# First two stages: whole-image evictions, the bias behind the convolution, rows by h mod 4, and every queue in program order

## The chip, the cores and the metric

The kernel runs on one core of a Trainium2 chip. The metric is the device time of one execution in microseconds (us).

## What is computed

The input is x, 16 images of 192 channels and 64x64 pixels, f32. Two layers follow each other:

```python
# layer 0
h = layernorm_over_channels(x) * w + b
projected, gate = split(conv1x1(h, 192 -> 384) + bias)
projected = depthwise3x3(projected)                    # zero padding
scanned = four recurrences s = d*s + (1-d)*cur of projected: along w, both ways, and along h, both ways, weighted by a softmax
local = depthwise3x3(projected)                        # other taps
mixed = (scanned + local) * sigmoid(gate)
bn = batchnorm(mixed)                                  # statistics over images and pixels
x = x + conv1x1(gelu(bn), 192 -> 192)
x = x + conv1x1(gelu(conv1x1(layernorm(x), 192 -> 768)), 768 -> 192)
# layer 1
t = relu(norm(mean_over_pixels(x) @ w1.T)); taps = t @ w2.T
out = depthwise 3x3 convolution of x with the image's own taps (four of nine) + bias
```

## The kernel before

A short **setup** (L73 to L195) computes the constants on the chip. Among them are the projection's weights with the norm's scale folded in and the channel mean taken out (wi), the bias broadcast over the partitions (bias_bc), the decay of each channel (dec_b), and for each channel the rows of the banded matrices that do a convolution or a recurrence along w as a matmul. The rows go to HBM (dv_d by L192, lv_d by L194, both on SP) and are read back in stage B shifted, as matrices.

**Stage A** (L197 to L265) is the layernorm's statistics and the 192 to 384 projection. Two images are worked on at once, one on partitions 0 to 63 and one on 64 to 127. An iteration takes 512 pixels of each, which is eight image rows in four groups of 128; there are 64 iterations, and four of them fill a block of 16 row pairs. load_a (L208) brings x in two DMAs of 384 KB on SP, two iterations ahead into three buffers. stat_a (L218) transposes 12 tiles on TensorE and takes mean and variance of each pixel on VectorE (L228, L229), then a root on ScalarE and a reciprocal. project (L235) does 12 matmuls of 384 columns in a group (L243) and evicts both images' results from one PSUM tile ps_pj (two of them in turn): the 192 projected channels by VectorE with the norm's factor and the bias (L246, the helper's line is L64), the 192 gate channels by ScalarE (L247). Both write every 16th element of a staging tile. After four iterations POOL's queue stores the staging tiles with four DMAs of 64 partitions (L252), 24 KB in one run for each partition. pg_d holds, for each image and row block, w, then the channel, then 16 rows of one parity of h.

**Stage B** (L268 to L398) goes through 24 groups of eight channels, four pairs in each; all 16 images are there at once, eight on each half of the partitions (partition = w). load_b (L285) brings a group's projected and gate values and its matrices, all on SP, one group ahead, in runs of 512 B. For a pair: depthwise (L305, seven parts with their edge cases, since rows lie by parity; 56 matmuls), copy from PSUM by ScalarE (q, L331), two decay tables by ScalarE (tab, L339), two scans along h by VectorE (L343, L345), local convolution and scans along w by matmuls (L352), sigmoid by ScalarE (L373), product and statistics by VectorE (L377, L378), and every four pairs a store by POOL's queue (L382). Then the batch norm's factors are made (L402 to L437), and the weights of stage C are loaded (L440 to L478).

**Stage C** (L481 to L695) has 64 chunks of 512 pixels of two images, in a software pipeline. load (L515) brings the chunk's x (two DMAs on SP, L520, two buffers) and, for every even chunk, y, the mixed values of two chunks (eight DMAs on SP, L528, one buffer). unmix transposes y on VectorE (L539), bn_gelu is L544 and L545 on ScalarE, out_proj multiplies and adds x on VectorE (L552, t = 0 to 2; the PSUM tile "a" has one buffer and is shared with the means ps_m and ps_v), center and normalize are the second layernorm (L563 to L581), first and second are the two large projections (L591 and L506, with gelu L594), final adds the result (L612). dynamic (L644 to L655) does layer 1 in pieces of 16 rows, and POOL's queue stores them.

What sets the order: Tile derives the waits and, on engines that are not named in manual_schedule, also the order of instructions in a block, by planned times. In stages A and B only TensorE keeps the order of the program (PE_ORDER, L62); in stage C TensorE, VectorE and ScalarE do. SP and POOL, whose queues only issue DMAs here, are ordered by the planner in all three. The loop of stage C starts:

```python
for n in range(-3, n_ch + 2):
    ...
    at(load, n + 3)
    at(unmix, n + 3)
    at(first, n, 0)
    at(bn_gelu, n + 3)
    at(out_proj, n + 2, 0)
    ...
    at(out_proj, n + 2, 2)
    at(second, n, 1)
```

Of the kernel before, what the change touches and what calls it, by code (L numbers as in the profile page):

```python
# [43 lines left out]
AR = CR // 2  # L44

# [7 lines left out]
def conv_block_kernel(ctx: ExitStack, tc: tile.TileContext, x, prm, w_in, w_out, w_fc1, b_fc1, w_fc2, w1, bn1, w2, out):  # L53
# [7 lines left out]
    PE_ORDER = {mybir.EngineType.PE}  # L61
# [14 lines left out]
    pg_d = dram.tile([n_img_all, NB, HW, 2 * C * BR], F32, tag="pg_d", name="pg_d")  # L76
# [7 lines left out]
    load_cls3(pt3, prm)  # L84

# [6 lines left out]
    eps5 = cp.tile([128, 1], F32, tag="eps5", name="eps5")  # L92
    nc.vector.memset(eps5, 1e-5)
# [3 lines left out]
    bias_bc = ce.tile([128, 2 * C], F32, tag="bias_bc", name="bias_bc")  # L97
    dec_b = ce.tile([128, 2, C // 2], F32, tag="dec_b", name="dec_b")
    stats = ce.tile([128, C, 6], F32, tag="stats", name="stats")


    with ExitStack() as stage:
        ka = stage.enter_context(tc.tile_pool(name="ka", bufs=1))
        wi = ka.tile([128, 3, 2 * C], F32, tag="wi", name="wi")
        load_cls3(wi, w_in)

        with tc.tile_pool(name="ps_set", bufs=1, space=PSUM) as ps0, tc.tile_pool(name="sset", bufs=1) as sp:
            lo = slice(0, 64)

# [21 lines left out]
            dg = sp.tile([64, 3, 4, 64], F32, tag="dg", name="dg")  # L131
            lnb = sp.tile([64, 3, 128], F32, tag="lnb", name="lnb")
            for t in range(3):
                for k, v in enumerate((pt3[lo, t, INB:INB + 1], pt3[lo, t, GTB:GTB + 1], dec[:, t, 2:3], dec[:, t, 3:4])):
                    nc.vector.tensor_scalar_mul(dg[:, t, k], ident[lo, lo], v)
                nc.vector.tensor_scalar_mul(lnb[:, t], ones[lo], pt3[lo, t, LN1B:LN1B + 1])
            pb = ps0.tile([128, 2 * C], F32, tag="pb", name="pb")
            for t in range(3):
                nc.tensor.matmul(pb, lnb[:, t], wi[lo, t], start=(t == 0), stop=False)
            for t in range(3):  # L140
                for k in range(2):
                    c0 = k * C + 64 * t
                    nc.tensor.matmul(pb[:, c0:c0 + 64], ones[lo], dg[:, t, k], start=False, stop=(t == 2 and k == 1))
            nc.vector.tensor_copy(bias_bc, pb)
            pd = ps0.tile([128, 2, C], F32, tag="pd", name="pd")
            for t in range(3):
                for k in range(2):
                    nc.tensor.matmul(pd[:, k, 64 * t:64 * t + 64], ones[lo], dg[:, t, 2 + k],
                                     start=(t == 0 and k == 0), stop=(t == 2 and k == 1))

            for i, q in enumerate(HALF):
                nc.vector.tensor_copy(dec_b[q].rearrange("p k (g c) -> p k g c", c=GC // 2),
                                      pd[q].rearrange("p k (g i c) -> p k g i c", i=2, c=GC // 2)[:, :, :, i])


            for t in range(3):
                nc.vector.tensor_scalar_mul(wi[:, t], wi[:, t], pt3[:, t, LN1W:LN1W + 1])
# [3 lines left out]
            for t in range(3):  # L161
                nc.tensor.matmul(pc, mean_w, wi[lo, t], start=(t == 0), stop=(t == 2))
            for t in range(3):
                nc.vector.tensor_sub(wi[:, t], wi[:, t], pc)
# [20 lines left out]
            gt = sp.tile([128, 8, C], F32, tag="gt", name="gt")  # L185
# [5 lines left out]
            for k in range(3):  # L191
                nc.sync.dma_start(dv_d[:, k].rearrange("g s c -> s g c"), gt[:, k].rearrange("s (g c) -> s g c", c=GC))  # L192
            for k in range(5):
                nc.sync.dma_start(lv_d[:, :, k].rearrange("g i s c -> s (g i) c"),  # L194
                                  gt[:, 3 + k].rearrange("s (g c) -> s g c", c=GC // 2))  # L195

        xp = stage.enter_context(tc.tile_pool(name="xa", bufs=3))  # L197
# [6 lines left out]
        xr = x.rearrange("b (t p) h w -> b p t (h w)", p=64)  # L204
# [3 lines left out]
        def load_a(n):  # L208
            p, c = divmod(n, NCH)
            xa = xp.tile([128, 3, CH], F32, tag="xa", name="xa")  # L210
            for i, q in enumerate(HALF):
                nc.sync.dma_start(xa[q], xr[2 * p + i, :, :, c * CH:(c + 1) * CH])
            ast[n]["xa"] = xa
# [4 lines left out]
        def stat_a(n):  # L218
# [5 lines left out]
            st6 = sp.tile([128, AR, 2, 6], F32, tag="st6", name="st6")  # L224
            mv = sp.tile([128, AR, 2, 2], F32, tag="mva", name="mva")
            for g in range(AR):
                for i, q in enumerate(HALF):
                    nc.vector.bn_stats(st6[:, g, i], xt[:, :, g, q])  # L228
                    nc.vector.bn_aggr(mv[:, g, i], st6[:, g, i])  # L229
            rs = sp.tile([128, AR, 2], F32, tag="rsa", name="rsa")  # L230
            nc.scalar.activation(rs, mv[:, :, :, 1], AF.Sqrt, bias=eps6)
# [3 lines left out]
        def project(n):  # L235
# [3 lines left out]
            for g in range(AR):  # L239
                ps = psa.tile([128, 2, CH], F32, tag="pj", name="ps_pj", bufs=2)  # L240
                for t in range(3):
                    for i, q in enumerate(HALF):
                        nc.tensor.matmul(ps[:, i, 0:2 * C], pixels(n, t, g)[q], wi[q, t], start=(t == 0), stop=(t == 2))  # L243
                for i in range(2):
                    j, r = part * AR + g, ast[n]["rs"][:, g, i:i + 1]
                    stt(stag[blk][i][:, 0:C, j], ps[:, i, 0:C], r, bias_bc[:, 0:C])  # L246
                    nc.scalar.activation(stag[blk][i][:, C:2 * C, j], ps[:, i, C:2 * C], AF.Identity, scale=r)  # L247
            if part == per - 1:
                p, jb = divmod(blk, NB // 2)
                for i in range(2):  # L250
                    for par, q in enumerate(HALF):
                        nc.gpsimd.dma_start(pg_d[2 * p + i, 2 * jb + par], stag[blk][i][q].rearrange("p o j -> p (o j)"))  # L252
                stag.pop(blk)

        with tc.manual_schedule(engines=PE_ORDER):
            for n in range(-1, n_ac):
                if n == -1:
                    load_a(0)
                    load_a(1)
                if 0 <= n and n + 2 < n_ac:  # L260
                    load_a(n + 2)
                if n + 1 < n_ac:
                    stat_a(n + 1)
                if n >= 0:
                    project(n)  # L265


    with ExitStack() as stage:  # L268
        kb = stage.enter_context(tc.tile_pool(name="kb", bufs=1))

        mask = kb.tile([128, 2, 2 * CH], F32, tag="mask", name="mask")
        nc.vector.memset(mask, 1.0)
        for k, r in ((0, 0), (1, HW - 1)):
            nc.vector.memset(mask[:, k].rearrange("p (i h) -> p i h", h=HW)[:, :, r:r + 1], 0.0)
# [6 lines left out]
        n_blk = n_half * NB  # L281
        grp = [dict() for _ in range(NCG)]
        bst = [dict() for _ in range(n_bp)]

        def load_b(g):  # L285
            s = grp[g]
            s["p"] = gp.tile([128, n_blk, GC, BR], F32, tag="pb", name="p_b")
            s["g"] = gp.tile([128, n_blk, GC, BR], F32, tag="gb", name="g_b")
            for k, dst in ((0, s["p"]), (1, s["g"])):
                lo = (k * C + g * GC) * BR  # L290
                for i, q in enumerate(HALF):
                    src = pg_d[i * n_half:(i + 1) * n_half, :, :, lo:lo + GC * BR]
                    nc.sync.dma_start(dst[q].rearrange("p n c j -> p n (c j)"), src.rearrange("i b w e -> w (i b) e"))
            s["dm"] = gp.tile([128, 3, HW, GC], F32, tag="dm", name="dm")
            s["lm"] = gp.tile([128, 5, HW, hp_], F32, tag="lm", name="lm")
            for i, q in enumerate(HALF):
                v = dv_d[g, :, 0:1, :]
                src = bass.AP(v.tensor, v.offset, [[GC, HW], [128 * GC, 3], [1, HW * GC]])
                nc.sync.dma_start(s["dm"][q].rearrange("p k m c -> p k (m c)"), src)
                v = lv_d[g, i, :, 0:1, :]  # L300
                src = bass.AP(v.tensor, v.offset, [[hp_, HW], [128 * hp_, 5], [1, HW * hp_]])
                nc.sync.dma_start(s["lm"][q].rearrange("p k m c -> p k (m c)"), src)
            s["o"] = gp.tile([128, n_blk, GC, BR], F32, tag="ob", name="o_b")

        def depthwise(k):  # L305
# [3 lines left out]
            ps = [psb.tile([128, CH], F32, tag="d", name="ps_d", bufs=4) for _ in range(2)]  # L309

            def part(di, src, dst, stop=False):
                for ih, q in enumerate(HALF):
                    for i, o in enumerate(HALF):
                        ch = c + hp_ * i
                        nc.tensor.matmul(dst(ps[ih][o]), s["dm"][q, di + 1, :, ch], src(s["p"][q, :, ch]),  # L315
# [3 lines left out]
            halves = lambda a: a.rearrange("p (b r) j -> p r b j", r=2)  # L319
            rows2 = lambda a: a.rearrange("p (b j r) -> p r b j", r=2, j=BR)  # L320
            edge = lambda a: a.rearrange("p r (i b) j -> p r i b j", b=2)
            part(0, halves, rows2)
            part(-1, lambda a: halves(a)[:, 0], lambda a: rows2(a)[:, 1])
            part(-1, lambda a: halves(a)[:, 1, :, 0:BR - 1], lambda a: rows2(a)[:, 0, :, 1:BR])
            part(-1, lambda a: edge(halves(a))[:, 1, :, 0, BR - 1], lambda a: edge(rows2(a))[:, 0, :, 1, 0])
            part(1, lambda a: halves(a)[:, 1], lambda a: rows2(a)[:, 0])
            part(1, lambda a: halves(a)[:, 0, :, 1:BR], lambda a: rows2(a)[:, 1, :, 0:BR - 1])
            part(1, lambda a: edge(halves(a))[:, 0, :, 1, 0], lambda a: edge(rows2(a))[:, 1, :, 0, BR - 1], True)
            q = wb.tile([128, 2, CH], F32, tag="q", name="q", bufs=3)
            for ih in range(2):  # L330
                nc.scalar.copy(q[:, ih], ps[ih])  # L331
            bst[k]["q"] = q

        def scans(k):
            q = bst[k]["q"].rearrange("p i n -> p (i n)")
            bst[k]["v"] = []
            for d in range(2):
                tab = wb.tile([128, 2 * CH], F32, tag=f"tab{d}", name=f"tab{d}")
                nc.scalar.activation(tab, mask[:, d], AF.Copy, scale=dec_b[:, d, k:k + 1])  # L339
# [25 lines left out]

        def gate(k):
            g, c = divmod(k, hp_)
            s = grp[g]
            for i in range(2):
                ch = c + hp_ * i  # L370
                o, n = s["o"][:, :, ch], g * GC + ch
# [366 lines left out]
```

## Time and profile before

| what | value |
|---|---|
| time, median of 3 runs | 4545.8 us (4540.98 to 4547.26) |
| profiled execution, its own time | 4551.3 us |
| its span | 4549.5 us |
| mean granted TensorE clock | 0.953 |
| busy in the span: TensorE, VectorE, ScalarE | 87%, 57%, 38% |
| setup, up to the first transposes | 0 to 80.2 us |
| stage A, up to the last eviction | 80.2 to 1028.4 us |
| stage B, first matmul to last statistics | 1081.3 to 1887.9 us |
| stage C | 1985.8 us (first L591) to the end |

A line of a profile names line, engine, operation and out<-in tiles, then busy time and mean time of one, and the idle time ahead of it with what ended it. "PEclk" and the clock column are the granted TensorE clock, in tenths or as a share. "SPq" is a DMA issue on SP's queue; its duration is that of issuing, not of the transfer.

### The profile page before, as it was taken

What the parts mean: (1) busy time and instruction counts of PE and PEld (TensorE: products, weight loads), DVE (VectorE), ACT (ScalarE), POOL (GpSimd) and SP (SyncE); (2) the same over time, 40 slices, a digit from 0 to 9 for tenths busy, and PEclk for the clock granted to TensorE, in tenths of its full rate; (3) what the DMA queues carried; (4) which work ended last, traced back from release to release, by engine and by line L of the source; (5) the groups of instructions that cost most, each with busy time, mean ns of one, the idle gap of its engine ahead of it and who ended that gap; (6) DMA issues with size and microseconds to landing.
All of it is one profiled execution on the core that took longest, in us unless ns stands there. A gap on an engine that the chain in (4) does not pass through costs nothing.

```text
span 4549.5 us, 58861 instructions
## 1 busy us (share of the span) xinstructions
PE 3950.4 (87%) x24876; PEld 1780.3 (39%) x24876; DVE 2593.3 (57%) x3832; ACT 1728.0 (38%) x2035; POOL 191.0 (4%) x316
## 2 busy tenths in 40 slices
PE   4677766674999999679999999999999999999994
PEld 2444444343555555323333333333333333333331
DVE  3444444443888888544456556466466565564654
ACT  1333333333555555323334333333333343343332
POOL 0000000000000000000000000000000000000001
PEclk9898888887999999779999999999999999999997
DMA  8665555559999999511112222122122122221212
GB/s 45 169 158 155 150 153 150 158 153 208 239 227 242 228 242 229 128 51 49 35 55 66 60 61 63 52 63 75 42 76 60 54 67 59 63 60 54 63 34 57
DMA packets 380295, 495.10 MB, mean 109 GB/s; under 512 B 54736, under 2 KB 267984, under 8 KB 375936
## 3 DMA queue, kind: packets, MB, share of 16 engines
q1 hardware_dynamic: 346496, 289.99, 28.9%
q0 software_dynamic: 33536, 201.35, 16.2%
q8 instruction: 196, 3.21, 0.3%
q14 instruction: 67, 0.55, 0.0%
HBM read 289.17 MB, written 202.11 MB: 108 GB/s over the span
## 4 chain that ended last, share of the span: by engine, by line
PE 55%; DVE 13%; ACT 4%; DMA 2%; issue 2%; SPq 1%; POOL 0%; ACTq 0%; POOLq 0%; DVEq 0%
PE ps_f L591 23%; PE ps_f L506 22%; PE ps_o L506 8%; DVE v L345 5%; DVE v L343 4%; DVE o_b L377 2%; ACT q L331 2%; ACT sg L373 2%; PE ps_m L506 1%; PE ps_v L506 1%; DVE stats L378 1%; DMA y<-mixed_d 1%; DMA pg_d<-stg 1%; DVE o L64 1%; SPq L528 0%
## 5 line engine op out<-in xcount | busy, mean ns | idle before, releaser
L591 PE MATMUL ps_f<-h,wf 64*128 64x512 f32 x4608 | 1042.5, 598 | 1.5 <-DVE h L581 1.5
L506 PE MATMUL ps_f<-gl,wf 128*64 128x512 f32 x4608 | 1021.5, 592 | 0.0
L594 ACT ACTIVATE gl<-ps_f,bf 128x1024 f32<-128x1024 f32 x384 | 422.1, 1111 | 709.2 <-PE ps_f L591 708.4
L591 PEld LDWEIGHTS ps_f<-h,wf 64*128 64x128 f32 x4608 | 430.2, 187 | 611.4 <-issue 607.4
L243 PE MATMUL ps_pj<-wi,xa 64*128 64x384 f32 x3072 | 560.0, 513 | 100.9 <-ACT stg L247 100.9
L506 PEld LDWEIGHTS ps_f<-gl,wf 128*64 128x64 f32 x4608 | 330.5, 137 | 658.9 <-issue 658.9
L552 DVE SCALAR_TENSOR_TENSOR ximg<-ps_o,pt,x 128x512 f32<-128x512 f32 x192 | 144.3, 752 | 660.9 <-PE ps_o L506 660.9
L243 PEld LDWEIGHTS ps_pj<-wi,xa 64*128 64x128 f32 x3072 | 300.5, 197 | 334.9 <-ACT stg L247 152.6
L64 DVE SCALAR_TENSOR_TENSOR stg<-ps_pj,rsa,bias_bc 128x192 f32<-128x192 f32 x512 | 266.6, 537 | 281.2 <-ACT stg L247 166.4
L64 DVE SCALAR_TENSOR_TENSOR o<-ximg,taps,o 128x1024 f32<-128x1024 f32 x288 | 369.3, 1284 | 93.6 <-ACT o L651 86.6
L506 PE MATMUL ps_o<-mx,wo 128*64 128x512 f32 x1536 | 380.9, 617 | 33.7 <-ACT mx L544 13.7
L247 ACT ACTIVATE stg<-ps_pj,rsa 128x192 f32<-128x192 f32 x512 | 288.9, 585 | 310.0 <-DVE stg L64 305.8
L315 PE MATMUL ps_d<-p_b,dm 64*64 64x256 f32 (+3 forms) x5376 | 300.9, 366 | 57.3 <-DMA dm<-dv_d 57.3
L339 ACT ACTIVATE tab<-mask,dec_b 128x1024 f32<-128x1024 f32 x192 | 220.4, 1150 | 319.0 <-DVE v L343 221.7
L315 PEld LDWEIGHTS ps_d<-p_b,dm 64*64 64x64 f32 x5376 | 267.4, 196 | 142.6 <-issue 139.6
L343 DVE TENSOR_TENSOR_SCAN v<-tab,q 128x1024 f32<-128x1024 f32 x96 | 220.0, 2292 | 175.9 <-ACT q L331 175.9
L223 PE MATMUL ps_xt<-ident,xa 128*128 128x128 f32 x768 | 119.4, 316 | 225.2 <-DMA xa<-in_x_dram 222.4
L580 DVE RECIPROCAL rs<-rs 128x512 f32<-128x512 f32 x64 | 214.6, 3353 | 170.2 <-ACT rs L579 170.2
L228 DVE BATCH_NORM_STATS2 st<-ps_xt 128x6 f32<-128x192 f32 x512 | 165.8, 336 | 245.8 <-PE ps_xt L223 187.6
L352 PE MATMUL ps_l<-q,lm 64*64 64x504 f32 (+1 forms) x2304 | 276.0, 604 | 2.8 <-ACT q L331 2.8
L568 ACT ACTIVATE sq<-h 128x1536 f32<-128x1536 f32 x64 | 94.9, 1483 | 465.8 <-DVE h L565 465.8
L352 PE MATMUL ps_l<-v,lm 64*64 64x512 f32 x1536 | 211.5, 617 | 66.3 <-DVE v L345 66.3
(132 smaller groups left out, 2936.8 us busy)
## 6 DMA issues: line engine op xcount, KB each, us to landing
pg_d<-stg POOLq DMA_DIRECT2D x64, 1536.0 KB, 19.0
xa<-in_x_dram SPq DMA_DIRECT2D x128, 384.0 KB
p_b<-pg_d SPq DMA_DIRECT2D x48, 1024.0 KB
g_b<-pg_d SPq DMA_DIRECT2D x48, 1024.0 KB
mixed_d<-o_b POOLq DMA_DIRECT2D x48, 1024.0 KB, 12.4
x<-in_x_dram SPq DMA_DIRECT2D x128, 384.0 KB
out_dram<-o POOLq DMA_DIRECT2D x192, 256.0 KB, 3.7
y<-mixed_d SPq DMA_DIRECT2D x128, 256.0 KB
```

Of the source, the lines that this page charges most:

```text
L64: nc.vector.scalar_tensor_tensor(o, in0, scalar, in1, ALU.mult, ALU.add, **kw)
L243: nc.tensor.matmul(ps[:, i, 0:2 * C], pixels(n, t, g)[q], wi[q, t], start=(t == 0), stop=(t == 2))
L247: nc.scalar.activation(stag[blk][i][:, C:2 * C, j], ps[:, i, C:2 * C], AF.Identity, scale=r)
L315: nc.tensor.matmul(dst(ps[ih][o]), s["dm"][q, di + 1, :, ch], src(s["p"][q, :, ch]), start=(di == 0), stop=stop)
L339: nc.scalar.activation(tab, mask[:, d], AF.Copy, scale=dec_b[:, d, k:k + 1])
L343: nc.vector.tensor_tensor_scan(vf, tab, q, 0.0, ALU.mult, ALU.add)
L345: nc.vector.tensor_tensor_scan(vf[:, ::-1], tab[:, ::-1], q[:, ::-1], 0.0, ALU.mult, ALU.add)
L352: nc.tensor.matmul(dst(bst[k]["ps"][i][o]), grp[g]["lm"][q, m, :, c], src(q, ih), start=start, stop=stop)
L506: nc.tensor.matmul(ps[q], w(i), rhs(i), start=start, stop=stop)
L580: nc.vector.reciprocal(rs, rs)
L591: nc.tensor.matmul(pf[:, i], wf1[q, t, 128 * m:128 * m + 128], s["h"][q, t], start=(t == 0), stop=(t == 2))
L594: nc.scalar.activation(gl, pf, AF.Gelu, bias=bf1[:, m:m + 1])
```

## The change

- All three stages now keep the program's order on five engines, SP and POOL among them (ORDER).
- Stage A: rows of a block are those with equal (h // 2) mod 2 taken in pairs, so that partition halves of the result hold h mod 4; x comes in runs of 512 B, six DMAs in an iteration, three for image 0 on SP and three for image 1 on ScalarE's queue, three iterations ahead into four buffers. Each image has its own PSUM tile (pj0, pj1): VectorE evicts all 384 channels of image 0, ScalarE those of image 1, without a bias. The next chunk's statistics are interleaved with the evictions. Stores go out over 128 partitions. pg_d is split in two tensors (groups 0 and 1, and 2 to 23), with projected and gate values of a group side by side.
- The projected channels' bias is added behind the depthwise convolution (bias_q), in the copy of q, with two further small activations for the image's edge rows. Its values are made by new code in the setup. The gate's bias stays in the sigmoid (bias_g).
- The vectors dv_d and lv_d are stored one by one in iterations 8 to 15 of stage A, and stage C's weights are loaded and prepared in iterations 3 and 16.
- Group 0 of stage B is fetched pair by pair during stage A on POOL's queue. In stage B a group's values come in runs of 1 KB, half 0 of the partitions on SP, half 1 on POOL's queue, likewise the stores; three buffers, in which the gate's product overwrites the projected values. depthwise has five parts (40 matmuls) and one PSUM tile of 1024 columns, and runs two pairs ahead. Tables, scans and sigmoids have places of their own in the loop; the mask is one row, broadcast.
- Stage C's code is the same but for the ORDER.

```diff
-    PE_ORDER = {mybir.EngineType.PE}
+    ORDER = {mybir.EngineType.PE, mybir.EngineType.DVE, mybir.EngineType.Activation, mybir.EngineType.SP,
+             mybir.EngineType.Pool}
...
-                nc.sync.dma_start(xa[q], xr[2 * p + i, :, :, c * CH:(c + 1) * CH])
+                for t in range(3):
+                    (nc.sync, nc.scalar)[i].dma_start(
+                        xa[q, t].rearrange("p (g n) -> p g n", n=128), xr[2 * p + i, u, :, t, part * AR:(part + 1) * AR])
...
-                ps = psa.tile([128, 2, CH], F32, tag="pj", name="ps_pj", bufs=2)
+                ps = [psa.tile([128, 2 * C], F32, tag=f"pj{i}", name=f"ps_pj{i}", bufs=2) for i in range(2)]
...
-                for i in range(2):
-                    j, r = part * AR + g, ast[n]["rs"][:, g, i:i + 1]
-                    stt(stag[blk][i][:, 0:C, j], ps[:, i, 0:C], r, bias_bc[:, 0:C])
-                    nc.scalar.activation(stag[blk][i][:, C:2 * C, j], ps[:, i, C:2 * C], AF.Identity, scale=r)
+                if n + 1 < n_ac:
+                    variance(n + 1, g)
+                j, rs = part * AR + g, ast[n]["rs"]
+                nc.vector.tensor_scalar_mul(stag[blk][0][:, :, j], ps[0], rs[:, g, 0:1])
+                nc.scalar.activation(stag[blk][1][:, :, j], ps[1], AF.Copy, scale=rs[:, g, 1:2])
...
+                for d, o0, o1 in ((0, 0, GF * 2 * GC), (1, GF * 2 * GC, 2 * C)):
+                    for i in range(2):
+                        nc.gpsimd.dma_start(pg_d[d][2 * p + i, 2 * u:2 * u + 2].rearrange("b w e -> (b w) e"),
+                                            stag[blk][i][:, o0:o1].rearrange("p o j -> p (o j)"))
...
-        with tc.manual_schedule(engines=PE_ORDER):
+        with tc.manual_schedule(engines=ORDER):
...
+                if 0 <= n and n + 3 < n_ac:
+                    load_a(n + 3)
...
+                if n == 3:
+                    load_weights()
+                if 8 <= n < 16:
+                    store_vectors(n - 8)
+                if n == 16:
+                    finish_weights(psa.tile([128, NFC], F32, tag="pb2", name="pb2"))
...
+            blocks = lambda a: a.rearrange("p (i b) j -> p i b j", b=NB)
+            rows4 = lambda a: a.rearrange("p (i j b) -> p i b j", b=NB, j=BR)
+            part(0, blocks, rows4)
+            part(-1, lambda a: blocks(a)[:, :, 0:NB - 1], lambda a: rows4(a)[:, :, 1:NB])
+            part(-1, lambda a: blocks(a)[:, :, NB - 1, 0:BR - 1], lambda a: rows4(a)[:, :, 0, 1:BR])
+            part(1, lambda a: blocks(a)[:, :, 1:NB], lambda a: rows4(a)[:, :, 0:NB - 1])
+            part(1, lambda a: blocks(a)[:, :, 0, 1:BR], lambda a: rows4(a)[:, :, NB - 1, 0:BR - 1], True)
...
-            for ih in range(2):
-                nc.scalar.copy(q[:, ih], ps[ih])
+            nc.scalar.activation(q, ps, AF.Identity, bias=bias_q[:, 0, k:k + 1])
+            for e, r in ((1, 0), (2, HW - 1)):
+                nc.scalar.activation(edge(q, r), edge(ps, r), AF.Identity, bias=bias_q[:, e, k:k + 1])
...
+            for k in range(-2, n_bp + 1):
+                if 0 <= k + 1 < n_bp:
+                    tables(k + 1)
                 if k >= 1:
                     vertical(k - 1)
                     gate(k - 1)
+                    if k % hp_ == 0 and k // hp_ + 2 < NCG:
+                        load_b(k // hp_ + 2)
+                if 0 <= k + 1 < n_bp:
+                    scans(k + 1)
+                if k + 2 < n_bp:
+                    depthwise(k + 2)
                 if 0 <= k < n_bp:
                     local(k)
+                    sigmoid(k)
...
-    with tc.manual_schedule(engines={mybir.EngineType.PE, mybir.EngineType.DVE, mybir.EngineType.Activation}):
+    with tc.manual_schedule(engines=ORDER):
```

## The prediction

> **What bounds the kernel now.** I read the slices of the page first, to find the stages, then busy time by stage, the waits within a stage, and last the order of work on each queue. The profiled execution took 4551.3 us, 5.5 above the median of 4545.8; its span is 4549.5. I make the sum in span time and add the difference to the median.
>
> ```profile
> PE   4677766674999999679999999999999999999994
> PEclk9898888887999999779999999999999999999997
> GB/s 45 169 158 155 150 153 150 158 153 208 239 227 242 228 242 229 128 51 49 35 55 66 60 61 63 52 63 75 42 76 60 54 67 59 63 60 54 63 34 57
> ```
>
> A slice is 113.7 us. Slices 2 to 9 (stage A) show PE at six to seven tenths and a clock below full; 10 to 16 (stage B) and 18 to 40 (stage C) show PE full. The stretches of A, B and C say it in us:
>
> ```profile
> 80.20:1028.70 948.50, 671.85 (x3840) 402.45 (x3840) 449.19 (x1603) 309.17 (x577) 33.06 (x62) 0.89 0.58 152
> 1100.00:1860.00 760.00, 695.24 (x8830) 423.46 (x8823) 644.42 (x552) 442.23 (x552) 49.39 (x46) 1.00 1.01 229
> 2000.00:4400.00 2400.00, 2395.54 (x11178) 866.39 (x11176) 1344.05 (x1449) 892.80 (x818) 87.15 (x164) 1.00 0.21 58
> ```
>
> After length come PE, weight loads, DVE, ACT, POOL, then clock, DMA share and GB/s. No engine fills A; two waits do:
>
> ```profile
> ACT stg L247 <- DVE stg L64: 305.8, 441, 2.9
> PE ps_xt L223 <- DMA xa<-in_x_dram: 169.5, 16, 13.6
> DVE stg L64 <- ACT stg L247: 166.4, 255, 0.7
> PE ps_pj L243 <- ACT stg L247: 100.9, 65, 1.9
> ```
>
> DVE and ACT take turns on one PSUM tile, and 16 times, once in nearly every 16-row block, PE waits for x while the block's store runs. In C PE has no idle time at all (2395.54 of 2400): whatever delays PE there is lost in full.
>
> **The change, part by part.**
>
> *Setup.* SP issues the first x at 73.74 because the vector stores stand before it (next fence); PE then waits to 80.2, while its own setup ended at 27.3 and DVE's at 24.9. The stores move to iterations 8 to 15 of A, one in each, so x is in flight from the start. New bias code adds some 60 small DVE and PE instructions; at 0.2 us each (the short DVE rows in C take 0.17 to 0.34) some 12 us, so the first transposes start at about 41: **-39** (bounds -20 to -50). In A the stores' 38 us lie on SP between loads that are issued three iterations (30 us) ahead; one store (about 7) fits in an iteration.
>
> ```profile
> 25.72 34.52 SPq L194 DMA_DIRECT2D lv_d<-gt  x5
> 73.74 3.91 SPq L212 DMA_DIRECT2D xa<-in_x_dram  x6
> ```
>
> *Stage A.* Per iteration (four row groups of two images, 64 in all, now 948.5/64 = 14.8 us) PE needs 2 x 4.14 us of projection and 1.53 us of transposes at full clock: 9.8 us, 39.2 per block of four. The eight pairs of half evictions (DVE 537 ns, ACT 585) become four DVE and four ACT evictions of 128x384. None such is in the trace: twice the 192 row is 1.08 and 1.17 us; the contiguous 128x512 rows (752, 577) scaled by 0.75 give 0.56 and 0.43. I take 0.87 and 1.0, nearer the strided rows, since the writes stay 16 floats apart. DVE then has 4 x 0.87 plus eight bn pairs of 0.33 plus 0.2, about 6.4 us; ACT 4.0 plus a root of 0.3 plus three DMA issues of 0.61, about 6.1. Both lie below PE's 9.8 and have a tile each, so the alternation goes. What is late next is x. Packets alternate: in the trace x issued at 444.16 landed only at about 464, under the store's 24 KB packets:
>
> ```profile
> 464.67 2.79 PE L223 MATMUL ps_xt<-ident,xa 128*128 128x128 f32 x12 [9.07 <-DMA xa<-in_x_dram]
> ```
>
> After, x is loaded three ahead instead of two, but in runs of 512 B instead of 2 KB, and 22 KB store packets still stand beside them; its second half is issued by ACT, where a held-up issue also holds the evictions behind it, and PE waits for those. A store of 6.3 MB at 300 to 380 GB/s lasts 17 to 21 us. Bounds per block: 40 (all hidden) and 58.9 (as now, from stores at 371.44, 432.42, 490.65, 552.01). I take 47, which keeps two fifths of the 19.7 that a block now takes beyond PE's 39.2: 16 x 47 + 5 for the start = 757, **-192** (-309 to 0).
>
> *Between A and B.* Now 52.5 us from A's last eviction (1028.4) to B's first matmul (1081.3): the last store lands 27.1 us after issue, then the first group loads at 217 GB/s. Group 0 is now fetched pair by pair inside A; only the last pair and the vectors remain: about 32, **-20** (0 to -35).
>
> *Stage B.* 96 channel pairs, 8.29 us each. PE works 7.55 and waits 0.73; DVE works about 7.1 and waits 1.19 for q:
>
> ```profile
> L343 DVE TENSOR_TENSOR_SCAN v<-tab,q 128x1024 f32<-128x1024 f32 x96 | 220.0, 2292 | 175.9 <-ACT q L331 175.9
> ```
>
> After, depthwise runs an iteration earlier, so that wait goes. PE is next: 56 depthwise matmuls with 1520 columns per quadrant take 3.08 us, 24 local ones with the same columns 2.81, so dropping 16 saves 16/32 of 0.27 = 0.13: 7.42. Two edge activations are added on ACT (4.8 us busy of 8.29, covered). I take 7.45: 96 x 0.84 = **-81** (-115 to 0: DVE's 7.1 alone, or DMA). Loads of both halves on two queues: 64-partition loads alone ran at 217 GB/s, loads and stores mixed at 382 to 389, and a group of 4 pairs moves 6.6 MB, 30 us at the first rate and 17 at the second, against 29.8 us of work.
>
> The Trainium skill ("SBUF — State Buffer", Door 1) says that PSUM has 8-byte cachelines and that any non-contiguous PSUM access slows matmuls significantly, which speaks against rows by h mod 4 (stride four instead of two). The rows don't show it for stride two: 589 ns for 64x512 with it, 582 to 635 for local's contiguous ones. By the rule B would gain nothing or lose, and the sum would be 81 higher or more.
>
> *Between B and C.* The weights (1900.4 to 1907.1 on SP) are loaded in A, but x and y are still awaited: 0.
>
> *Stage C.* Its code stays, PE, DVE and ACT keep their order, but SP now follows the program. Before, the scheduler put y's eight DMAs right after the transposes that free y, ahead of the next even x; y was then used an iteration (38.8 us) later. In program order y stands behind the even chunk's x, and that x waits for the residual add L552, t=2, of two chunks earlier, the end of the iteration. The trace has the moment:
>
> ```profile
> 2602.12 0.75 DVE L552 SCALAR_TENSOR_TENSOR ximg<-ps_o,pt,x 128x512 f32<-128x512 f32 x1 [1.35 <-PE ps_o L506]
> 2602.90 1.25 SPq L520 DMA_DIRECT2D x<-in_x_dram  x2
> 2603.51 2.88 DVE L539 STREAM_TRANSPOSE mx<-y 128x512 f32<-128x512 f32 x3
> 2606.42 12.46 SPq L528 DMA_DIRECT2D y<-mixed_d  x8
> 2614.48 0.75 DVE L552 SCALAR_TENSOR_TENSOR ximg<-ps_o,pt,x 128x512 f32<-128x512 f32 x1 [8.09 <-PE ps_o L506]
> ```
>
> After, the x of an even chunk is issued at 2602.90, y from 2604.2, while the transposes of just that y are next on DVE. Where y was awaited at once, its third part was used 25.7 and 27.3 us after the first issue (1942.02 to 1967.72; 1910.86 to 1938.19). So y lands near 2630.6, the transposes end at 2631.6, and behind them on DVE stands L552 of t=0, which frees the single PSUM tile "a": 2632.5. The mean's matmul L506 ps_m, which needs that tile, ran at 2619.41. PE stands still 13.1 us. Idle time also costs clock: after waits of about 12 us the next matmuls ran slow (24 of L591 7.11 us against 5.42, ps_m 1.98 against 1.03), 2.65 us. That makes 15.75 us for each pair of chunks, 30 pairs in steady state: **+472** (30 x 11 to 17.5: +330 to +525).
>
> **Sum.** -39 - 192 - 20 - 81 + 472 = +140. On the median: 4545.8 + 140 = **4686 us**.
>
> **Rivals.**
> 1. *A becomes PE-bound* at 40 us per block: for it, three loads ahead are 30 us and the store lasts 21; against it, x starves now under the same packets. 4686 - 117 = 4569. With C's wait at its low end (13.1 without the clock, 393) 4490.
> 2. *A stays bound by DMA* at 58: 4686 + 176 = 4862; for it, 512 B runs.
> 3. *y isn't late in C*, the other side: its DMAs are reached early enough, or land sooner. All 472 go: 4214. For it: DVE waits for y only 33.7 us, 5 times, now. Against it: the order of SP is fixed by the program and x's wait is in the trace. The point of decision is the delay per pair: at 332/30 = 11.1 us C's loss equals the gain of A, B and setup, below that the change is faster.
> 4. *Stride-four PSUM writes slow depthwise*: at twice its 3.08 us and less overlap, 2.5 us per pair of channels more, 96 x 2.5 = +240: 4926.
>
> **Chances.** Forecast 0.56 (own range 4600 to 4760), rival 1 0.20 (a third of it faster), rival 2 0.10, rival 3, or y half as late, 0.11, rival 4 0.03. Leaving out rival 3, rival 4 and half of rival 2: 4490 to 4800. Measurement can tell 0.2%, 9 us, from no change. Faster: 0.11 + 0.07 = 0.18; within 0.2%: 0.04; slower: 0.78.
>
> **What would show it.** Right: in C, DVE idle before L539 with "DMA y" as releaser, 30 times some 20 us, PE below 0.9 there and clock below 1.00, y issued after the even x; A's stores 47 us apart with waits on x left and the alternation of L64 and L247 gone; B's period near 7.45 with no wait for q; first transposes near 41. Wrong: L539 without idle time (rival 3), stores 40 apart (1) or 58 (2), depthwise over 3.1 us (4). The forecast fails most cheaply by the size of C's delay: every us of it per pair is 30 us.

## The result and the profile after

The changed kernel took 4719.6 us (median of 4 runs, 4707.3 to 4723.1) against 4545.4 for the kernel before in the same runs: 1.038 times as long, 95% interval 1.0358 to 1.0401. The forecast was 4686 (4490 to 4800). Its profiled execution has a span of 4721.3 us, 171.8 longer than before. By stage, from the first and last instructions of each (the last eviction of the kernel before starts at 1028.4 and ends at 1028.9, which is the end taken here):

| stretch | before, us | after, us | difference | forecast |
|---|---|---|---|---|
| start to first transposes | 80.2 | 35.9 | -44.3 | -39 |
| A, to its last eviction | 948.7 | 718.6 | -230.1 | -192 |
| last eviction to B's first matmul | 52.4 | 26.0 | -26.4 | -20 |
| B, to its last statistics | 806.5 | 837.8 | +31.3 | -81 |
| last statistics to C's first large projection | 97.9 | 98.4 | +0.5 | 0 |
| C | 2563.7 | 3004.6 | +440.9 | +472 |

So C gives back more than A, the setup and the gap gained together (441 against 301), and B, which was to be faster, is slower. These are the same slices as were shown of before (118 us each now), from the page of the changed kernel:

```profile
PE   6888996988888658988988898888978997998894
PEclk9999997999999878998999899989999998999897
GB/s 136 175 219 204 243 245 224 215 225 221 226 219 214 152 52 28 34 35 57 59 37 59 55 47 45 63 47 43 59 60 36 56 61 35 60 51 46 53 34 58
```

In A (up to slice 7) PE is now at eight to nine tenths, where it was at six to seven. In C, from slice 15 on, most slices show eight tenths where nearly all showed nine, and the clock falls below full. The stretches of A, B and C, with the same columns as before (length, busy time of PE, weight loads, DVE, ACT, POOL, clock, DMA share, GB/s):

```profile
35.85:754.60 718.75, 640.89 (x3876) 394.02 (x3876) 456.66 (x1350) 239.39 (x322) 37.34 (x70) 0.95 0.73 210
860.00:1600.00 740.00, 636.54 (x6851) 451.63 (x6847) 596.62 (x514) 501.32 (x602) 74.32 (x83) 0.93 0.98 220
1800.00:4500.00 2700.00, 2356.86 (x10606) 842.15 (x10604) 1282.97 (x1383) 853.44 (x774) 83.32 (x156) 0.93 0.19 50
```

PE was busy in 99.8% of C and is in 87%; its clock went from 1.00 to 0.93. The waits of the changed kernel name what is late in each stage:

```profile
DVE mx L652 <- DMA y<-mixed_d: 756.2, 96, 10.8
PE ps_d L450 <- DMA dm<-dv_d: 143.8, 22, 27.1
PE ps_pj L359 <- ACT stg L365: 67.3, 15, 17.5
ACT stg L365 <- DMA xa<-in_x_dram: 44.8, 4, 14.0
```

The first is C's (it was 33.7 us in 5 times before, at C's start alone), the second B's, the others A's. The alternation of the two evictions is gone from the list. C's moment, which the prediction worked out, looks like this in the timeline (L633 and L641 issue x and y, L652 transposes y, L665 is the residual add; a row with x4 holds the two DMAs of two chunks, and of this one the second pair, the even chunk's, went out at 2675.01):

```profile
2636.18 40.08 SPq L633 DMA_DIRECT2D x<-in_x_dram  x4
2674.22 0.75 DVE L665 SCALAR_TENSOR_TENSOR ximg<-ps_o,pt,x 128x512 f32<-128x512 f32 x1 [1.35 <-PE ps_o L619]
...
2676.42 12.09 SPq L641 DMA_DIRECT2D y<-mixed_d  x8
2686.12 1.04 DVE L652 STREAM_TRANSPOSE mx<-y 128x512 f32<-128x512 f32 x1 [10.41 <-DMA y<-mixed_d]
2691.24 1.04 DVE L652 STREAM_TRANSPOSE mx<-y 128x512 f32<-128x512 f32 x1 [4.08 <-DMA y<-mixed_d]
2701.53 1.03 DVE L652 STREAM_TRANSPOSE mx<-y 128x512 f32<-128x512 f32 x1 [9.26 <-DMA y<-mixed_d]
2702.49 0.71 DVE L665 SCALAR_TENSOR_TENSOR ximg<-ps_o,pt,x 128x512 f32<-128x512 f32 x1
2703.26 1.98 PE L619 MATMUL ps_m<-sm,mean_bd 128*64 128x512 f32 x4 [11.56 <-DVE ximg L665]
2705.17 7.31 PE L704 MATMUL ps_f<-h,wf 64*128 64x512 f32 x24
```

y is issued 2.2 us after the residual add of the iteration before, its third part is used 25.1 us later, and PE stands still 11.56 us and is then slow for two groups (1.98 us for 1.03, 7.31 for 5.42). That it is x that holds y shows in the next pair of chunks:

```profile
2729.02 2.89 DVE L652 STREAM_TRANSPOSE mx<-y 128x512 f32<-128x512 f32 x3
2768.64 14.15 SPq L641 DMA_DIRECT2D y<-mixed_d  x8
```

y's buffer is free at 2731.9, when these transposes end, and the next y goes out 36.7 us later, right behind the even chunk's x (issued at 2767.22, after the residual add of 2766.44).

### The profile page after: what moved, and what is told of

The parts are those of the page before. It is cut to its first block, busy times and chain, and to the rows that moved or that the text cites. A ratio compares the mean times of both kernels' runs of the same rounds, so it can differ in the third digit from the quotient of the medians.

```text
span 4721.3 us, 55898 instructions
## 1 busy us (share of the span) xinstructions
PE 3985.1 (84%) x23368; PEld 1847.6 (39%) x23368; DVE 2599.7 (55%) x3627; ACT 1764.3 (37%) x1875; POOL 230.6 (5%) x375
## 4 chain that ended last, share of the span: by engine, by line
PE 53%; DMA 21%; issue 13%; SPq 9%; DVE 3%; POOL 1%; ACT 1%; ACTq 0%; DVEq 0%; POOLq 0%
PE ps_f L704 20%; PE ps_f L619 14%; DMA y<-mixed_d 9%; DMA dm<-dv_d 8%; SPq L641 8%; PE ps_o L619 6%; PE ps_l L494 4%; PE ps_d L450 3%; PE ps_m L619 2%; DMA mixed_d<-pg_o 1%; DMA mixed_d<-pg_e 1%; PE ps_v L619 1%; PE ps_pj L359 1%; DVE ximg L665 1%; SPq L633 1%
## 5 line engine op out<-in xcount | busy, mean ns | idle before, releaser
L704 PE MATMUL ps_f<-h,wf 64*128 64x512 f32 x4608 | 1097.2, 624 | 1.5 <-DVE h L694 1.5
L704 PEld LDWEIGHTS ps_f<-h,wf 64*128 64x128 f32 x4608 | 451.0, 197 | 669.3 <-issue 633.1
L652 DVE STREAM_TRANSPOSE mx<-y 128x512 f32<-128x512 f32 x192 | 191.9, 1025 | 756.2 <-DMA y<-mixed_d 756.2
L619 PE MATMUL ps_m<-sm,mean_bd 128*64 128x512 f32 x256 | 95.2, 832 | 377.6 <-DVE ximg L665 377.6
L365 ACT ACTIVATE stg<-ps_pj,rsa 128x384 f32<-128x384 f32 x256 | 233.9, 925 | 473.0 <-PE ps_pj L359 344.0
L665 DVE SCALAR_TENSOR_TENSOR ximg<-ps_o,pt,x 128x512 f32<-128x512 f32 x192 | 143.0, 745 | 424.6 <-PE ps_o L619 424.6
L364 DVE TENSOR_SCALAR stg<-ps_pj,rsa 128x384 f32<-128x384 f32 x256 | 226.3, 884 | 198.4 <-PE ps_pj L359 198.0
L450 PE MATMUL ps_d<-pg_o,dm 64*64 64x384 f32 (+2 forms) x2560 | 210.5, 468 | 84.3 <-DMA dm<-dv_d 84.3
L768 POOL DMA_DIRECT2D out_dram<-o x192 | 102.5, 538 | 2967.8 <-DVE o L66 2964.7
L450 PEld LDWEIGHTS ps_d<-pg_o,dm 64*64 64x64 f32 x2560 | 169.3, 201 | 153.8 <-issue 129.1
L485 DVE TENSOR_TENSOR_SCAN v<-tab,q 128x1024 f32<-128x1024 f32 x96 | 218.3, 2274 | 16.2 <-ACT tab L473 16.2
L487 DVE TENSOR_TENSOR_SCAN v<-tab,q 128x1024 f32<-128x1024 f32 x96 | 217.5, 2266 | 0.0
```

The lines of the kernel that those rows point to most:

```text
L364: nc.vector.tensor_scalar_mul(stag[blk][0][:, :, j], ps[0], rs[:, g, 0:1])
L365: nc.scalar.activation(stag[blk][1][:, :, j], ps[1], AF.Copy, scale=rs[:, g, 1:2])
L450: nc.tensor.matmul(dst(ps[o, ih]), s["dm"][q, di + 1, :, ch], src(s["pg"][q, :, 0, ch]), start=(di == 0), stop=stop)
L485: nc.vector.tensor_tensor_scan(vf, tab, q, 0.0, ALU.mult, ALU.add)
L487: nc.vector.tensor_tensor_scan(vf[:, ::-1], tab[:, ::-1], q[:, ::-1], 0.0, ALU.mult, ALU.add)
L619: nc.tensor.matmul(ps[q], w(i), rhs(i), start=start, stop=stop)
```

## The experiments

Theory: in C the order of SP alone costs the time (y behind an x that waits); A gains from the eviction and from x; B is held by its loads. The rivals were that the fixed order of POOL or the new layout costs C its time, that only one of A's parts counts, and for B several about its queues. The first experiments test C in both directions, and A's two parts alone. A kernel's stage lengths and waits below are those of its profiled execution.

### y_first: the changed kernel with y ahead of x

```diff
-        x2 = xp.tile([128, 3, CH], F32, tag="x2", name="x2")
-        for i, q in enumerate(HALF):
-            nc.sync.dma_start(x2[q], xv[2 * p + i, :, lo:hi].rearrange("(t p) n -> p t n", p=64))
         if c % 2 == 0:
...
             ys[n // 2] = y
+        x2 = xp.tile([128, 3, CH], F32, tag="x2", name="x2")
+        for i, q in enumerate(HALF):
+            nc.sync.dma_start(x2[q], xv[2 * p + i, :, lo:hi].rearrange("(t p) n -> p t n", p=64))
```

> The changed kernel; in stage C's load the eight DMAs of y stand ahead of the two of the even chunk's x, SP still in program order. My theory: C is 441 us longer only because y stands behind that x, which waits for L552 (t=2); y's own release, the transposes that free it, comes an iteration earlier. Then y is issued right after those transposes, VectorE no longer waits for it, a pair of chunks takes 77.6 us again instead of 92.2, and the time falls by about 440, to 4280 (4265 to 4300). Rival: the fixed order as such, POOL's queue included, or the other memory layout of C's tiles costs the time; then it stays near 4720, or between the two.

Measured: 4261.5 us, 0.936 of before (0.935 to 0.938), 458 less than the changed kernel. C takes 2564.6 us, as before, which is 440 of the 458; DVE waits for y 33.0 us, 5 times. Its issues on SP, one pair of chunks, show y out ahead of the even chunk's x (the x4 in the middle are an even and an odd chunk's, issued at 2351.64 and 2390.47, each right after an L665):

```profile
2313.72 12.43 SPq L638 DMA_DIRECT2D y<-mixed_d  x8
2351.64 40.07 SPq L642 DMA_DIRECT2D x<-in_x_dram  x4
2394.00 12.20 SPq L638 DMA_DIRECT2D y<-mixed_d  x8
```

and the stretch of C has PE full and the clock at 1.00 again:

```profile
1800.00:4100.00 2300.00, 2295.53 (x10724) 830.47 (x10724) 1297.31 (x1403) 858.82 (x786) 86.50 (x162) 1.00 0.22 58
```

SP is in program order here as well, so it is not the fixed order that costs, but which of two DMAs comes first in it.

### order_in_c_only: the kernel before with SP's order

```diff
-    with tc.manual_schedule(engines={mybir.EngineType.PE, mybir.EngineType.DVE, mybir.EngineType.Activation}):
+    with tc.manual_schedule(engines={mybir.EngineType.PE, mybir.EngineType.DVE, mybir.EngineType.Activation, mybir.EngineType.SP}):
```

> The kernel before; its only edit is SP added to the engines that keep program order in stage C. My theory: the same wait for y appears with nothing else of the change, so the time rises by about 440 to 4985 (4960 to 5010), with VectorE waiting for y some 750 us and the granted clock in C near 0.93. Rival: the wait needs the other parts of the change (the layout of mixed_d, its writers on two queues, POOL's order); then it stays at 4545.

Measured: 4992.5 us, 1.097 (1.095 to 1.098), +442.7 on 4549.7. The group of the transposes has the wait, with nothing else of the change in the kernel:

```profile
L539 DVE STREAM_TRANSPOSE mx<-y 128x512 f32<-128x512 f32 x192 | 191.9, 1026 | 751.4 <-DMA y<-mixed_d 751.4
```

One name in a set of engines is worth 443 us, and the rival (layout, queues of the writers, POOL) is out.

### evict_per_image, x_three_ahead and evict_and_x_ahead: A's parts in the kernel before

```diff
-                ps = psa.tile([128, 2, CH], F32, tag="pj", name="ps_pj", bufs=2)
+                ps = [psa.tile([128, 2 * C], F32, tag=f"pj{i}", name=f"ps_pj{i}", bufs=2) for i in range(2)]
...
-                for i in range(2):
-                    j, r = part * AR + g, ast[n]["rs"][:, g, i:i + 1]
-                    stt(stag[blk][i][:, 0:C, j], ps[:, i, 0:C], r, bias_bc[:, 0:C])
-                    nc.scalar.activation(stag[blk][i][:, C:2 * C, j], ps[:, i, C:2 * C], AF.Identity, scale=r)
+                j, rs = part * AR + g, ast[n]["rs"]
+                nc.vector.tensor_scalar_mul(stag[blk][0][:, :, j], ps[0], rs[:, g, 0:1])
+                nc.scalar.activation(stag[blk][1][:, :, j], ps[1], AF.Copy, scale=rs[:, g, 1:2])
```

is the first; the second is xa bufs 3 to 4 and load_a(n + 3) for load_a(n + 2); the third has both.

> The kernel before; stage A's eviction alone is changed: one PSUM tile for each image, VectorE evicts 384 channels of image 0 and ScalarE those of image 1. The projection's bias of the first 192 channels is left out. Loads, stores and layout stay as before. Theory 1 (the eviction gives most of A's 230 us): an undisturbed iteration falls from 11.5 to 9.4 us, but x still starves behind the store, 9 us in each block, so a block takes about 39 + 10 = 49 instead of 58.9: 16 x 10 = -160, about 4385. Theory 2 (x is what holds A, and the alternation hides under it): blocks stay near 57, at most -40, about 4510.

> The kernel before; x of stage A goes to four buffers and is loaded three iterations ahead instead of two, all else as before (2 KB runs, both halves on SP). Theory 1 (x starves only because it is issued too late): the 169 us of waits for x in A go, blocks fall from 58.9 to about 47 (four iterations of 11.5), about 4385. Theory 2 (the store's 24 KB packets hold x back as long as they run, however early it is issued): a third of it at most, about 4500. With both this and the eviction alone known, their sum against A's 230 us shows whether the parts add.

> The kernel before with the two edits of evict_per_image and x_three_ahead together, the bias of the first 192 channels left out; runs of 2 KB, loads on SP, stores over 64 partitions and the layout stay. Theory 1 (these two are all of A's gain, and what is left is PE): blocks of 40, 19 us less than before, 4548 - 300 = 4248 (4235 to 4275). Theory 2 (without the stores over 128 partitions and the shorter runs, x is late again once the iterations are short: three iterations are then 28 us of lead): the two gains of 70 and 178 add at best, blocks of 43 to 46, 4300 to 4340.

Measured: 4479.8 (0.985, 0.983 to 0.986), 4371.8 (0.961, 0.959 to 0.962) and 4357.7 (0.956, 0.955 to 0.958). Against their runs of before that is -70, -178 and -198. The expectations for the third were both wrong in size: the parts don't add up, and the second part's block of 47.7 us stays 47.7 with both. Together they bring A from 948.7 us to 753.0, 196 of the 230 that it gained. The waits of evict_per_image and then of evict_and_x_ahead in A say why:

```profile
PE ps_xt L223 <- DMA xa<-in_x_dram: 269.1, 18, 52.3
```

```profile
PE ps_xt L223 <- DMA xa<-in_x_dram: 148.8, 20, 54.6
```

In both the two evictions no longer wait for each other, and PE waits for x instead. (One wait of 52 to 55 us in each is that of the setup; what is left is 217 and 94 us, against 169.5 before. With x three ahead alone it is 5 us, and the alternation stays.) Faster iterations make three of them a lead of 28 us, and the store is as long as it was: 30 to 34 us from the first of its four issues to the last landing. What the changed kernel has beyond these two parts is, among others, the store over 128 partitions, which takes 18 to 25 us: its packets of 22 KB take 0.87 us each in the trace (26 GB/s from one of the 16 engines), those of 24 KB from 64 partitions 1.51 us (16 GB/s). Its later blocks take 36 to 43 us, but for one of 48.6. That it is this, and not the runs of 512 B or the second queue, wasn't tried by itself.

### x_on_sp and weights_late: what is left in A

Both start from y_first. The first issues all of x on SP; the second moves load_weights from iteration 3 to 35, store_vectors from 8 to 40 and finish_weights from 16 to 48.

> The kernel of y_first, with all six DMAs of an iteration's x on SP, none on ScalarE's queue. My theory: in stage A the evictions stand still because a load that ScalarE has to issue is held up ahead of them (its waits of 17 and 13 us), and PE waits some 60 us for ScalarE's evictions; with the issue on SP only x itself has to be in time, and three iterations of lead cover it: A shorter by 30 to 60, 4215 (4200 to 4235). Rival: the transfer is what is late, not the place of its issue; then PE waits as long for x, and the time stays at 4262, or rises, since SP then issues 3.7 us of loads in each 9.4 us iteration.

> The kernel of y_first, with stage C's weights loaded in iteration 35 instead of 3 and made ready in 48 instead of 16, and the vectors stored in iterations 40 to 47 instead of 8 to 15. Theory 1 (the moved loads and stores with their 16- and 32-byte packets make the slow blocks of A): the blocks of 57, 52 and 57 us at 142, 238 and 298 us move to the iterations from 35 on, the early ones fall to 40, and the time stays within 20 of 4262. Theory 2 (A's first blocks are slow by themselves, while its queues fill): the blocks stay where they are.

Measured: 4277.6 (0.940, 0.939 to 0.942), 16 slower than y_first (A takes 718.8 us for 712.4), and 4266.4 (0.938, 0.936 to 0.940), the same as y_first. The first expectation fell: PE's waits for ScalarE's evictions are gone, and it waits for x itself instead, 77.3 us in 24 times. The place of the issue moves the wait and doesn't make it:

```profile
PE ps_xt L335 <- DMA xa<-in_x_dram: 77.3, 24, 15.7
```

In the second the slow blocks moved with the work. POOL issues the stores at the end of a block; in weights_late the early ones stand 38 to 43 us apart, and the ones from iteration 36 on up to 59:

```profile
162.86 2.14 POOL L370 DMA_DIRECT2D pg_d<-stg  x4 [37.34 <-DVE stg L364]
201.69 2.14 POOL L370 DMA_DIRECT2D pg_d<-stg  x4 [36.70 <-DVE stg L364]
...
509.59 2.15 POOL L370 DMA_DIRECT2D pg_d<-stg  x4 [42.78 <-DVE stg L364]
564.60 2.29 POOL L370 DMA_DIRECT2D pg_d<-stg  x4 [52.87 <-DVE stg L364]
623.68 2.15 POOL L370 DMA_DIRECT2D pg_d<-stg  x4 [56.09 <-DVE stg L364]
```

So the work that was taken out of the setup and out of B's end is paid in A, and not while A's queues fill.

### dm_before_pg, b_queues_as_before, store_from_constant and contiguous_values: B

All with y ahead of x. dm_before_pg sends dm ahead of a group's values and lm behind them; b_queues_as_before has, beside that, all loads on SP and the stores on POOL's queue; store_from_constant, from dm_before_pg, sends a constant tile in the stores; contiguous_values, from moved_work_spread (below), reads 32 KB in a run for each partition.

```diff
-                    src = pg_d[d][i * n_half:(i + 1) * n_half, :, :, lo:lo + GE]
...
+                        run = n_blk * GE
+                        v = pg_d[1]
+                        src = bass.AP(v.tensor, v.offset + (2 * (g - GF) + i) * 64 * run, [[run, 64], [1, run]])
```

> The kernel of y_first; in stage B's load the matrices dm of a group go ahead of its values, and lm behind them, on the same two queues. My theory: PE's waits for dm (129 us, 22 times, 27 of them at B's start) are the length of one queue's chain: store of a half, its landing, 2 MB of values at about 190 GB/s while that half is alone, then dm. With dm sent while the store lands, the chain is some 4 us shorter for each group: -60 to -90, 4185 (4165 to 4210). Rival: B is bound by the DMA engines' throughput (their share is 0.98 and 216 GB/s are moved); then the order of the same bytes changes nothing, and the time stays at 4262, with PE waiting for the values instead of dm.

> As dm_before_pg, but with both halves of stage B's loads on SP and the stores on POOL's queue, as in the kernel before. Theory 1 (two queues are worth having, since halves of the partitions then move side by side at 380 GB/s): B is slower than in dm_before_pg by 3 to 6 us a group, +70 to +140. Theory 2 (the halves hardly ever move side by side, since each queue waits for its own store; and stores on a queue of their own land sooner): the same as dm_before_pg or up to 40 faster.

> The kernel of dm_before_pg, but stage B's stores send a small constant tile in place of the gate's product: the same bytes in the same runs go to HBM, their content is constant, and what C reads is not the mixed values. A group's buffer is then free for the next load as soon as VectorE has read it, without waiting for the store's landing. My theory (the chain of store, landing and load on each queue is what is late): PE's waits for values in B, 57 + 30 us in dm_before_pg, fall below 20, and B goes to some 28 us a group, -70, 4150 (4130 to 4175). Rival (the DMA engines' throughput, share 0.96 to 0.98): the same bytes take as long, and the time stays at 4222.

> The kernel of moved_work_spread, but from group 2 on stage B's loads of values read 32 KB in one run for each partition instead of 32 runs of 1 KB; the bytes are as many and each is read once, but they lie elsewhere, so channels and pixels are mixed up and the output isn't the reference's. Theory 1 (what bounds B is the rate at which runs of 1 KB are read, 188 GB/s for one half alone and some 240 for both): the loads go faster, PE's waits for values (84 us) go and a group takes 28 us: -70 to -90, 4110. Theory 2 (the bound is on the side of the 64 partitions written, or the bytes as such): less than 30 of it, 4165 to 4195.

| kernel | time, us | to before | B, first matmul to last statistics |
|---|---|---|---|
| y_first | 4261.5 | 0.936 (0.935 to 0.938) | 830.1 |
| dm_before_pg | 4222.1 | 0.928 (0.927 to 0.930) | 790.4 |
| b_queues_as_before | 4237.8 | 0.932 (0.929 to 0.934) | 806.9 |
| store_from_constant | 4226.2 | 0.927 (0.926 to 0.929) | 800.5 |
| moved_work_spread | 4192.6 | 0.920 (0.919 to 0.921) | 786.2 |
| contiguous_values | 4185.8 | 0.921 (0.919 to 0.922) | 778.7 |

B took 806.5 us before and 837.8 in the changed kernel. dm_before_pg gained 39, half of what the chain theory said, which puts B 16 us below the kernel before, and PE waits for the values in place of dm:

```profile
PE ps_d L451 <- DMA pg_o<-pg_d: 57.4, 11, 13.2
PE ps_d L451 <- DMA pg_e<-pg_d: 30.1, 7, 6.3
```

store_from_constant decides against that theory: nothing waits for a store's landing, the loads of both halves are issued within half a microsecond on the two queues (1020.94 on SP, 1021.32 on POOL), and B is no shorter. What hardly moves is the rate: over the whole of B the kernels of the table move 216 to 231 GB/s, the kernel before 223 and the changed one 214. contiguous_values shows that the length of the runs doesn't set it: a packet of 32 KB takes 2.46 us, 13.3 GB/s for an engine, one of 1 KB 0.083 us, 12.3, and B is within 8 us. Stretches of 3 us in B of the changed kernel show the two rates that the prediction took as its ends:

```profile
1106.00:1109.00 3.00, 3.00 (x35) 1.89 (x32) 3.00 (x2) 3.00 (x5) 0.00 (x0) 1.00 1.15 189
1109.00:1112.00 3.00, 3.00 (x51) 2.32 (x48) 2.93 (x6) 1.99 (x3) 0.00 (x0) 1.00 1.09 219
1112.00:1115.00 3.00, 3.00 (x36) 1.86 (x32) 3.00 (x3) 2.97 (x5) 0.00 (x0) 1.00 1.03 370
```

The DMA share is above 1 in each (overlapping packets count twice), so the share doesn't tell these rates apart: 189 GB/s move while SP's load of half 0 runs alone, 219 with POOL's load of lm into half 1 beside it (the 4 KB packets of POOL's queue before 1112 are 0.33 MB, which is lm's half), and 370 beside POOL's store of half 1. Where both halves' loads of values run at once (store_from_constant, 1031 to 1040 us), 236 GB/s move. A second queue is worth little to two loads, though theory 1 of b_queues_as_before is not quite out: one queue costs B 16 us more. Whether one load into all 128 partitions would be faster than two into 64 was not tried, so it stays open what holds B's rate.

This is where a rule of the Trainium skill would have helped ("SBUF — State Buffer", "Can I just issue two DMAs to hit both halves?"): it says that two DMAs on the two halves of the partitions serialize, measured there at 6% over one. The loads here agree in the main: two together moved 219 to 236 GB/s, one alone 189 here and 217 in the kernel before, so that the second adds 1 to 25% and is far from doubling the rate.

### moved_work_spread: A's moved work in the gaps of the stores

From dm_before_pg; vectors and weights go out in the second and third iteration of blocks 1 to 7.

```diff
-                if n == 3:
-                    load_weights()
-                if 8 <= n < 16:
-                    store_vectors(n - 8)
...
+                m, r = divmod(n, per)
+                if r in (1, 2) and 1 <= m < 5:
+                    store_vectors(2 * (m - 1) + r - 1)
+                if r in (1, 2) and 5 <= m < 8:
+                    load_weights(2 * (m - 5) + r - 1)
```

> The kernel of dm_before_pg, with the vectors' stores and the weights' loads not one iteration after the other but in the second and third iteration of a block, when the block's store has left most of the DMA engines: vectors in blocks 1 to 4, weights in blocks 5 to 7, made ready in iteration 48. Theory 1 (they cost because they meet the block's store, whose packets already hold x back): the slow blocks of 50 to 60 us fall to some 43, A by 40, 4180 (4165 to 4200). Theory 2 (their small packets take the same time from x wherever they are): the same 4222.

Measured: 4192.6 us, 0.920 (0.919 to 0.921), 30 below dm_before_pg; the last store of A leaves at 718 instead of 755. It is the fastest of the kernels that leave nothing out, 363 us below the kernel before in the same runs and 527 below the changed one.

## Why the prediction was right, point by point

- **The sum**: +172 us of span for +140. That it came so near is in part luck. B was 112 too high, and A, C, the setup and the gap were together 81 lower than forecast (38, 31, 5 and 6). That the change is slower doesn't rest on this: C's term alone outweighs all the others.
- **C, the deciding term**: right in mechanism and size. Forecast 15.75 us for a pair of chunks; the pair takes 92.2 us (y at 2676.42 and 2768.64) for 77.6: 14.6, of which 11.56 is PE's wait (forecast 13.1) and 2.84 the slow clock after it (2.65). The wait is 1.5 us shorter, mostly since y's third part was used 25.1 us after the first issue instead of 26.4. Shown in both directions by order_in_c_only (+443) and y_first (-458, 440 of it in C).
- **A**: -230 for -192. The step "x is late next" held, and its place, too: ScalarE's held-up issue (waits of 17.5 and 13.0 us) stops the evictions. But it does so in the blocks with the moved weights and vectors; the others come near PE's 39.2. The forecast's 47 is close to the mean of 44.9 (718.6/16) by another route: it spread one loss over all blocks, and left out that moved work costs anything there, so the nearness of the two is luck. (The upper bound, 58.9, is the stage's length shared out over 16 blocks; the four stores named for it stand 60.2 us apart on average.) x_on_sp shows that the transfer is the cause and the issue only its place.
- **Eviction**: 884 and 925 ns measured for 870 and 1000; the alternation went, as said.
- **Setup, gap**: -44 for -39, -26 for -20.
- **B**: the one term with the wrong sign, +31 for -81. The work was taken too high: where nothing is late a pair takes 7.0 us, not 7.45, with VectorE full. And the step "a group of 4 pairs moves 6.6 MB, 30 us at the first rate and 17 at the second, against 29.8 us of work" failed. A group moves 7.7 MB: values and store come to 6.3, dm and lm add 1.4, most of which I left out. It takes 34.9 us, 220 GB/s (the trace has 214 over the whole of B, whose first groups are loaded earlier). The forecast's 29.8 us would need 258 GB/s by the same count, and the fastest here, contiguous_values with 32.4 us a group, comes to 238. I took the mixed rate of loads and stores, which was in the trace, for what loads on two queues would reach; what B comes to is near the first of the two, the 64-partition rate of 217. I also gave no price to dm's place behind a group's values on the same queues, and dm_before_pg shows that it is worth 39 us. Neither run size nor the wait for the stores was what mattered.
- **The rule on strided PSUM access** that the prediction weighed: in a stretch without waits (1451 to 1473 us) a 64x512 matmul with stride four takes 589 ns, as it did with stride two before, and local's contiguous ones 598. The 40 of a depthwise take 2.85 us for the 3.08 of the 56 before, local's with as many contiguous columns 2.80. So this case shows no slowing by the stride, and rival 4's 2.5 us are out.
- Of the rivals, 1 was half right (blocks of 40 where nothing is moved in), 2 and 3 wrong.

## What to carry to other kernels

Before a queue is put in program order, write its instructions in that order beside what each waits for: an instruction that waits for the end of an iteration holds every transfer behind it, and the one that is needed next must stand ahead of it. Where transfers set the pace, as in B, less work on the engines shortens the stage little: count all of a group's bytes, at a rate that loads alone were seen to reach. Two loads into the two halves of the partitions were at most a quarter faster than one here, and the DMA share doesn't show the room that is left: it was about 1 at 189 GB/s and at 370. Work moved out of a setup isn't gone where the next stage's transfers are what is late.

## What I had not expected

A store from 128 partitions moved 26 GB/s for each engine, one from 64 partitions 16, with packets of nearly the same size; I take this for what lets x through in stage A, though it wasn't tried by itself. And the length of a run, 1 KB or 32 KB, made little difference to a load into 64 partitions (12.3 and 13.3 GB/s for each engine, 8 us of B).
